# Earlier dilation start, half-graph blocks, first removals inside the slots and later chunk stores in a fused four-layer graph kernel

## The chip, the cores and the metric

The kernel runs on one core of one Trainium2 chip. The metric is the device time of one execution in microseconds (us), lower is better; a time without a profile is the median of several runs. A core has TensorE (PE; its weight loads are listed as PEld), VectorE (DVE), ScalarE (ACT), GpSimd (POOL), and a queue, SP, from which most plain transfers are issued. GpSimd's queue issues transfers too: here all those that change the type of the data.

## The reference, cut to what matters

There are 16 graphs of 1024 nodes with 128 features, and four layers with a layer norm behind each. Layer 0 is attention masked by the adjacency; layer 1 a maximum over neighbours; layer 2 a sum over neighbours with a two-stage perceptron; layer 3 first thins out ("dilates") the adjacency row by row and then runs three passes of neighbour means and a batch norm over all graphs.

```python
def _dilate_pattern(adj_bool, mask_b):
    def step(carry, n):
        row = jnp.take(carry, n, axis=0)
        nbi = row.astype(jnp.int32)
        num = jnp.sum(nbi)
        sf = jnp.where(num > T_DIL, (num + K_DIL - 1) // K_DIL, 1)
        rank = jnp.cumsum(nbi)
        rm = row & (rank % sf == 0)
        valid = (mask_b[n] != 0) & (num > 1)
        rm = jnp.where(valid, rm, False)
        keep = ~rm
        carry = carry.at[n].set(row & keep)
        carry = carry.at[:, n].set(carry[:, n] & keep)
        return (carry, None)
    out, _ = jax.lax.scan(step, adj_bool, jnp.arange(N))
    return out
...
x = _layernorm(x + _L0_gnn_ref(x, adj, Wv, bv, Wk, bk, Wq, bq))
x = _layernorm(x + _L1_gnn_ref(x, adj, W, b))           # max over j of relu(p_i + q_j + b) * adj_ij
x = _layernorm(x + _L2_gnn_ref(x, adj, nodemask, W1, b1, W2, b2, eps))
x = _layernorm(x + _L3_gnn_ref(x, adj, nodemask, ...))  # dilate(adj), then 3 x (sage, relu, batch norm)
```

The dilation depends on the adjacency alone, not on the features, so it can run beside layers 0 to 2. But row n of a graph depends on the removals of all rows before it.

## The kernel before, in words

**Stages.** A prologue computes graph 0's attention. Then a loop of *slots* computes layer 1 for all graphs, and in its gaps layers 0 and 2 and the dilation. After the slots a *bridge* finishes layer 2 of the last graph and begins layer 3, and a tail does layer 3's three passes.

**Slots (L927).** `for s in range(-2, B * NP)`: each graph has NP = 86 slots, 1376 in all, and each slot has two halves of 512 nodes. In a half, `look_up` (L843) makes four TensorE products into one of two PSUM tiles `pg`, and VectorE takes the running maximum into `best` (L908). What the products need is prepared two slots ahead: `count` (product L812, ScalarE L813), `table` (L824, L827) and `low_part` (L832, L834). The subset counts read a chunk `AT` of the transposed adjacency; each chunk serves PC = 10 slots.

**Transfers in the slots.** `load_columns(at)` (L753) is called every ten slots, for a chunk two chunks ahead. It issues the load of chunk `at` on GpSimd (L764, float32 to fp8, four buffers), and on SP the store of the chunk before it, `at - 1`, to `adj8` (L758), from which layer 3 reads later. `load_x` (L747) fetches the features of the next graph on SP, in three buffers; `load_rows` (L751) the adjacency rows `An` on GpSimd.

**Streams.** Other work is written as generators: `attend` and `scores` (layer 0 of the next graph), `tables_of` (layer 1's tables), `rest` (norm of layer 1 and all of layer 2 for the graph before). At each step a generator yields `ask(engine, cost, ...)`. `advance` lets it go on when there is `room` on that engine in this half slot, when its delay is over, and when one of the two shared PSUM banks is free. So the order on each engine is written at build time by costs, not by measured times.

**Dilation (generator `dilation`).** It runs over K = 32 blocks of R = 32 rows, for all 16 graphs at once. For a block, VectorE prepares counts (`spread`, `low_counts`, `rest`, L655), then GpSimd runs a chain of 31 rows (L669 to L679), 10 small instructions each, every row depending on the one before. The result `hit` goes to DRAM and back in another layout on SP (L686, L689), VectorE transposes it to `hit_T` (L703), GpSimd computes thresholds (L707 on), and the next block can begin. In `remove`, four column groups per block follow: TensorE ranks (L599), ScalarE `rank` (L601), VectorE `gone` (L613, two buffers), SP stores of `gone` to `removed` (L615) and of a transposed part to `removed_T` (L622). `prepare` loads and counts the block after.

`dilate_on` (called once in each half slot) takes the dilation's next step once `due` is no later than the present slot, and adds to `due` what the step yields: 1.03 slots for a row, and for the yield ahead of `hit_T` a number that makes a whole block last `(B * NP - 10) / K` = 42.69 slots. `due` starts at 0, so block 0 begins in slot 0.

**What sets the order of the work.** In the slots and the bridge, TensorE, ScalarE, VectorE and GpSimd run in the order written (`manual_schedule`). SP is not on that list: the scheduler orders SP's transfers itself when the kernel is built, by its own estimate of when each can go. [...]

**Bridge (L930 to L975).** When the slots are over, the rest of the dilation generator is run, its pool is closed, `first_weights` loads layer 3's weights, `load_near` and `load_gone` fetch the stored adjacency of graphs 0 and 1 and the removals of graph 0. `rest(B - 1)` is taken in pieces (`go_on(n)`), with graph 0's removals between: `both_halves` (products L1008 and L1010 into `pgone`, VectorE `near` L1014), then `degrees` (L1026, ACT copy L1027), `expanded` (fp8 to float32 copies, L1050), `settle` (1/degree on VectorE), and behind the last norm six chunks of graph 1.

Of the kernel before, what the change touches and what calls it, by code (L numbers as in the profile page):

```python
# [40 lines left out]
P = 128  # L41
T = N // P
# [32 lines left out]
def tile_graph_layers(ctx: ExitStack, tc, a, out):  # L75
# [166 lines left out]
    def layers_012():  # L242
# [3 lines left out]
        psum = psums.enter_context(tc.tile_pool(name="psumA", bufs=1, space=PSUM))  # L246
        apool = es.enter_context(tc.tile_pool(name="apool", bufs=1))
        w4 = es.enter_context(tc.tile_pool(name="w4", bufs=1))
        dil = right.enter_context(tc.tile_pool(name="dil", bufs=1, side="right"))
        w2 = right.enter_context(tc.tile_pool(name="w2", bufs=1, side="right"))  # L250
        steps = dil.tile([P, 512 + P], BF, name="steps")
        nc.vector.memset(steps, 1.0)
        upto, beyond = steps[:, :512], steps[:, P:]
# [246 lines left out]
        def dilation():  # L500
# [134 lines left out]
            for k in range(K):  # L635
# [59 lines left out]
                if k + 1 < K:  # L695
# [2 lines left out]
                    at = dil.tile([P, Q, R], F32, name="at_columns", tag="far")  # L698
                    nc.vector.tensor_tensor_scan(at.rearrange("p q m -> p (q m)"), running.rearrange("p q m -> p (q m)"),
                                                 near.rearrange("p q m -> p (q m)"), 0.0, op0=ALU.mult, op1=ALU.add)  # L700
                yield (B * NP - 10) / K - 36.93, 0.65, False
                hit_T = dil.tile([P, Q, R], BF, name="hit_T")
                nc.vector.transpose(hit_T.rearrange("p q m -> p (q m)"), hit_p.rearrange("p q m -> p (q m)"))  # L703
                cut(E[:, :, own], hit_T, counts[:, 3, :])
# [37 lines left out]
            for cost, gives in behind:  # L742
                yield 0.5, cost, gives

        def load_x(b):
            X[b] = apool.tile([P, T, D], F32, name="X", bufs=3)
            nc.sync.dma_start(out=X[b], in_=x[b].rearrange("(t p) d -> p t d", p=P))  # L747
# [4 lines left out]

        def load_columns(at):  # L753
            b, c = divmod(at, T + 1)
            if at:
                before, k = divmod(at - 1, T + 1)
                rows = min(CH, N - k * CH)
                nc.sync.dma_start(out=adj8[before][k * CH:k * CH + rows], in_=AT[at - 1][:rows])  # L758
            if b < B:
                rows = min(CH, N - c * CH)  # L760
                t = AT[at] = apool.tile([CH, N], F8, name="AT", bufs=4)
                if rows < CH:
                    nc.gpsimd.memset(t, 0.0)
                nc.gpsimd.dma_start(out=t[:rows], in_=adjT[b, c * CH:c * CH + rows])  # L764
# [89 lines left out]
        def dilate_on():  # L854
            nonlocal due, wants_bank
            if due <= now and not (wants_bank and taken >= 2 and given.get(taken - 2, 1e9) > now):
                after, cost, wants_bank = next(dilate, (B * NP, 0, False))
                due += after
                room["V"] -= cost

        def slot(s, last):

            nonlocal now
            now = s
            b, g = divmod(s, NP)
            if s >= 0 and g == 0:
                bests[b] = bests[b - 1] if b else w4.tile([P, 2, N], F32, name="best")
                if b + 1 < B:
                    start(tables_of(b + 1), True)
                    load_x(b + 1)  # L870
                    start(attend(b + 1))
                    start(scores(b + 1))
            if s >= 0 and g % PC == 0 and b * (T + 1) + g // PC + 2 <= B * (T + 1):
                load_columns(b * (T + 1) + g // PC + 2)
            for h in range(2):
                now = s + 0.5 * h
                for e in ROOM:
                    room[e] = min(room[e] + ROOM[e] / 2, ROOM[e] / (2 if e in ("PE", "V") else 1))
                if s >= 0:
                    pg = psum.tile([P, 2, 512], F32, tag="wide", name="pg", bufs=2)  # L880
                    look_up(s, h, pg)
                early = s >= 0 and due < now
                if early:
                    dilate_on()
                advance(("PE",))
                advance(("A", "V", "Pool"))
                if s >= 0 and not early:
                    dilate_on()
                if h == 0 and s % 2 and s + 1 < last:
                    low_part(s + 1)  # L890
                if s + 2 < last:
                    count(s + 2, h)
                    if h and s % 2 == 0:
                        table(s + 2)
                if s >= 0:
                    own = bests[b][:, :, halves[h]]
                    if g == 0:
                        if b:
                            if h:
                                merge(b - 1, h)  # L900
                            total(b - 1, h)
                        nc.vector.tensor_copy(own, pg)
                        if b and h:
                            start(rest(b - 1))
                    else:
                        if g == NP - 1 and h:
                            merge(b, 0)
                        nc.vector.tensor_max(own, own, pg)  # L908
            if s >= 0:
                hots.pop(s)  # L910

        dilate = dilation()
        due, wants_bank = 0.0, False
        load_x(0)
        for at in range(2):
            load_columns(at)
# [1 line left out]
        for t in range(T):  # L918
            while ("e", 0, t) not in happened:
                next(front)  # L920
            for what in back:
                if what[5] == ("e", 0, t + 1):
                    break
        for _ in front:
            pass
        first = tables_of(0)
# [3 lines left out]
        with tc.manual_schedule(engines={mybir.EngineType.PE, mybir.EngineType.Activation, mybir.EngineType.DVE,  # L930
                                         mybir.EngineType.Pool}):
            for s in range(-2, B * NP):
                slot(s, B * NP)
            total(B - 1, 0)
            merge(B - 1, 1)
            total(B - 1, 1)
            assert not streams, streams
            for _ in dilate:
                pass
            right.close()  # L940
            first_weights()
            nears[0], nears[1] = load_near(0), load_near(1)
            gones[0] = load_gone(0)
            last = rest(B - 1)

            def go_on(n):
                for _ in range(n):
                    next(last, None)

            def both_halves(b, c):  # L950
                p = psum.tile([P, 2, 512], F32, tag="wide", name="pgone", bufs=2)
                for h in range(2):
                    removals(p[:, h], b, c, h)
                keep(b, nears[b][:, c, :], p.rearrange("p a n -> p (a n)"))

            go_on(27)
            for c in range(T):
                both_halves(0, c)
            go_on(5)
            nc.sync.dma_start(out=kept[0], in_=nears[0])  # L960
            gones[1] = load_gone(1)
            go_on(18)
            p = psum.tile([P, 2, 512], F32, tag="wide", name="pdeg", bufs=2)
            degrees(0, [p[:, h] for h in range(2)])
            go_on(12)
            expanded(0, range(T))
            go_on(12)
            settle(0)
            for _ in last:
                pass  # L970
            for c in range(6):
                both_halves(1, c)
            psums.close()
            psum = ctx.enter_context(tc.tile_pool(name="psum", bufs=2, space=PSUM))

# [40 lines left out]
    def one_half(b, i):  # L1016
# [2 lines left out]
        removals(p, b, c, h)  # L1019
        keep(b, nears[b][:, c, halves[h]], p)  # L1020

    def degrees(b, ps):
        deg = ep.tile([1, N], F32, name="deg")
        for p, s in zip(ps, halves):
            for c in range(T):
                nc.tensor.matmul(p, ones_b, nears[b][:, c, s], start=(c == 0), stop=(c == T - 1))  # L1026
            nc.scalar.copy(deg[:, s], p[0:1, :])  # L1027
        nc.sync.dma_start(out=degree[b], in_=deg)
        d = dues[b] = ep.tile([T, P], F32, name="deg_t", bufs=2)
        nc.sync.dma_start(out=d, in_=degree[b].rearrange("(t i) -> t i", t=T))  # L1030
# [15 lines left out]
    def expanded(b, chunks):  # L1046
        m = ms.setdefault(b, [])
        for c in chunks:
            m.append(ep.tile([P, N], F32R, name="m", bufs=10))
            nc.scalar.copy(m[c], nears[b][:, c, :])  # L1050
        return m

# [135 lines left out]
        nc.sync.dma_start(out=hidden[l][b], in_=R3[b])  # L1188
        nc.sync.dma_start(out=around[b], in_=convolve(r, m, part))

    ep = None
    Wr = Wx = bs = gs = bes = Wl = bl = None

    def first_weights():
        nonlocal ep, Wr, Wx, bs, gs, bes, Wl, bl
        ep = ctx.enter_context(tc.tile_pool(name="ep", bufs=1, side="right"))
        Wr, Wx, bs, gs, bes = ([f(f"L3_gnn_{w}{l}", pool=ep, queue=nc.sync) for l in (1, 2, 3)] for w, f in (
            ("Wr", weight), ("Wx", weight), ("b", column), ("g", column), ("be", column)))
        Wl = weight("L3_gnn_Wl", (P, 3, P), ("(c p) o -> p c o", {"p": P}), ep, nc.sync)
# [112 lines left out]
    def summed(b):  # L1312
        hs = []
        for l in range(2):
            r = ep.tile([P, N], F32, name="m", bufs=10)
            nc.sync.dma_start(out=r, in_=hidden[l][b])
            hs.append(r)
        p = wide("pl")
# [7 lines left out]
    o = summed(0)  # L1326
    for b in range(B):
        following = summed(b + 1) if b + 1 < B else None
        xb = ep.tile([P, T, D], F32, name="xb", tag="m", bufs=10)
        nc.sync.dma_start(out=xb, in_=x3[b])  # L1330
        for h in range(2):
            p = rows_bank("pback")
# [38 lines left out]
```

## Time and profile before

| | us |
|---|---|
| three runs | 6195.82, 6211.70, 6206.11 |
| median | 6206.11 |
| the profiled execution, its own time | 6199.75 |
| its span in the trace | 6198.0 |
| first look-up product (L843) / first maximum (best) | 133.2 / 140.0 |
| last maximum of the slots ends | 5088 |
| first neighbour product of layer 3 (L1071) begins | 5159.9 |
| tail from there to the end | 1038 |

The whole slot stage takes most of the time: 1376 slots in 4955 us. Its engines, per stretch (start and end in us, length, then busy us and number of instructions of PE, PEld, DVE, ACT and POOL, then TensorE's granted clock, the share of the DMA engines, GB/s). The four stretches are a piece of the first two graphs, one of graph 8, one of graph 11 and one of the last:

```profile
200.00:550.00 350.00, 316.24 (x1731) 167.12 (x1742) 306.55 (x434) 241.06 (x453) 246.86 (x863) 0.95 0.22 27
2624.00:2925.00 301.00, 278.45 (x1590) 148.90 (x1597) 268.48 (x400) 214.00 (x410) 215.91 (x724) 1.00 0.23 33
3538.00:3863.00 325.00, 287.11 (x1591) 153.01 (x1597) 268.76 (x400) 212.07 (x409) 219.98 (x730) 0.94 0.20 30
4798.00:5089.00 291.00, 242.99 (x1254) 111.98 (x1257) 240.53 (x290) 173.34 (x325) 182.25 (x622) 0.91 0.09 20
```

In the profile, L12 is line 12 of the kernel; `out<-in` are tile names; `x` is a number of instructions. A wait is listed as "engine line <- who ended the wait". Idle time of an engine that is not on the path to the end costs nothing.

### The profile page before, as it was taken

What the parts mean: (1) busy time and instruction counts of PE and PEld (TensorE: products, weight loads), DVE (VectorE), ACT (ScalarE), POOL (GpSimd) and SP (SyncE); (2) the same over time, 40 slices, a digit from 0 to 9 for tenths busy, and PEclk for the clock granted to TensorE, in tenths of its full rate; (3) what the DMA queues carried; (4) which work ended last, traced back from release to release, by engine and by line L of the source; (5) the groups of instructions that cost most, each with busy time, mean ns of one, the idle gap of its engine ahead of it and who ended that gap; (6) DMA issues with size and microseconds to landing.
All of it is one profiled execution on the core that took longest, in us unless ns stands there. A gap on an engine that the chain in (4) does not pass through costs nothing.

```text
span 6198.0 us, 93287 instructions
## 1 busy us (share of the span) xinstructions
PE 5582.7 (90%) x30144; PEld 3046.0 (49%) x30250; DVE 4870.0 (79%) x7484; ACT 3988.2 (64%) x7362; POOL 3613.1 (58%) x11879
## 2 busy tenths in 40 slices
PE   5989899989898989999989798989999878999998
PEld 4545454545454545454545454545444435555654
DVE  3888788888888888889888788888889875555455
ACT  3767676767676767677767576767666554344855
POOL 2676666667666767677777757667677651110114
PEclk8999999989999999999999899999999989999999
DMA  5021213121212212122121211212121014554645
GB/s 42 11 33 25 40 22 42 22 40 24 40 24 31 32 32 32 32 32 38 26 43 22 39 24 31 31 31 33 31 33 28 19 41 124 159 144 133 214 163 191
DMA packets 496976, 334.28 MB, mean 54 GB/s; under 512 B 303338, under 2 KB 448228, under 8 KB 492388
## 3 DMA queue, kind: packets, MB, share of 16 engines
q1 hardware_dynamic: 405504, 260.29, 14.5%
q0 software_dynamic: 89008, 67.42, 12.6%
q8 instruction: 237, 3.88, 0.3%
q14 instruction: 255, 2.09, 0.1%
q10 hardware_dynamic: 1972, 0.59, 0.1%
HBM read 362.38 MB, written 133.96 MB: 80 GB/s over the span
## 4 chain that ended last, share of the span: by engine, by line
PE 31%; DVE 10%; ACT 4%; POOL 3%; issue 2%; DMA 1%; SPq 0%; DVEq 0%; POOLq 0%; ACTq 0%
PE pg L843 7%; PE pagg L1071 5%; DVE best L908 5%; PE pm L812 3%; PE po L1101 2%; PE po L1095 1%; PE pa L439 1%; PE pav L397 1%; PE pp L300 1%; ACT hot L813 1%; PE pdeg L1026 1%; DVE near L1014 1%; PE psc L349 1%; PE prank L599 1%; PE pe L387 1%
## 5 line engine op out<-in xcount | busy, mean ns | idle before, releaser
L908 DVE TENSOR_TENSOR best<-best,pg 128x1024 f32<-128x1024 f32 x2720 | 3259.3, 1214 | 512.6 <-PE pg L843 501.7
L813 ACT ACTIVATE hot<-pm,one_less 128x512 fp32r<-128x512 f32 x2752 | 1887.4, 689 | 780.5 <-PE pm L812 773.2
L843 PE MATMUL pg<-hot,high 64*128 64x512 f32 x5504 | 1407.3, 508 | 258.9 <-DVE best L908 220.8
L843 PE MATMUL pg<-hot,low 64*128 64x512 f32 x5504 | 1115.5, 402 | 0.0
L812 PE MATMUL pm<-AT,lit 120*128 120x512 fp8e4 x2752 | 1085.9, 395 | 4.5 <-ACT low L834 3.5
L843 PEld LDWEIGHTS pg<-hot,high 64*128 64x128 f32 x5504 | 523.5, 187 | 1014.6 <-DVE best L908 492.8
L669 POOL TENSOR_SCALAR sc<-low_counts,half_mask,rest 16x1 f32<-16x1 f32 x992 | 354.4, 357 | 393.9 <-DVE rest L655 283.2
L843 PEld LDWEIGHTS pg<-hot,low 64*128 64x128 f32 x5504 | 537.9, 192 | 0.0
L812 PEld LDWEIGHTS <-lit 120*128 120x128 fp8e4 x2752 | 270.3, 98 | 389.8 <-issue 313.5
L674 POOL TENSOR_SCALAR sc<-sc 16x1 f32<-16x1 f32 x992 | 393.1, 396 | 105.1
L834 ACT CAST low<-pt 128x256 fp32r<-128x256 f32 x688 | 256.0, 372 | 263.3 <-PE pt L832 261.9
L671 POOL TENSOR_SCALAR sc<-sc 16x1 f32<-16x1 f32 x992 | 324.5, 327 | 107.6
L1116 POOL TENSOR_TENSOR length<-length,mhalf 128x8 f32<-128x8 f32 x48 | 78.9, 1644 | 489.2 <-DVE length L1115 489.2
L676 POOL TENSOR_SCALAR hit<-V,sc 16x31 bf16<-16x31 bf16 (+30 forms) x992 | 362.4, 365 | 0.0
L677 POOL TENSOR_SCALAR last_rank<-V,sc 16x31 f32<-16x31 bf16 (+30 forms) x992 | 342.9, 346 | 0.0
L832 PE MATMUL pt<-high,less 128*128 128x256 f32 x688 | 279.2, 406 | 67.6 <-ACT high L827 61.5
L824 PE MATMUL pt<-ident,sub 128*128 128x128 f32 x1376 | 277.5, 283 | 51.8 <-ACT hot L813 50.0
L486 DVE TENSOR_TENSOR sub<-sub,q 128x24 f32<-128x24 f32 (+11 forms) x768 | 304.0, 397 | 24.8 <-ACT q L304 10.4
L397 PE MATMUL pav<-v,eT 128*128 128x128 f32 x2048 | 301.5, 292 | 2.0 <-ACT eT L390 2.0
L397 PEld LDWEIGHTS pav<-v,eT 128*128 128x128 f32 x2048 | 255.4, 196 | 73.3 <-issue 55.7
L670 POOL TENSOR_SCALAR sc<-sc 16x1 f32<-16x1 f32 x992 | 237.0, 239 | 86.5
L349 PE MATMUL psc<-kT,qT 128*128 128x256 f32 x1024 | 276.3, 388 | 9.9 <-issue 9.9
(270 smaller groups left out, 9662.9 us busy)
## 6 DMA issues: line engine op xcount, KB each, us to landing
removed<-gone SPq DMA_DIRECT2D x128, 256.0 KB
An<-in_adj_dram POOLq DMA_DIRECT2D x16, 1024.0 KB, 16.0
E<-in_adj_dram POOLq DMA_DIRECT2D x128, 128.0 KB, 6.6
gone_all<-removed POOLq DMA_DIRECT2D x64, 256.0 KB, 10.2
near<-adj SPq DMA_DIRECT2D x16, 1024.0 KB
kept<-near SPq DMA_DIRECT2D x16, 1024.0 KB
share<-share SPq DMA_DIRECT2D x32, 512.0 KB
hidden<-r SPq DMA_DIRECT2D x32, 512.0 KB
```

The costliest lines, as they stand in the source:

```text
L349: nc.tensor.matmul(psc[:, 256 * i:256 * (i + 1)], qT[:, t * P:(t + 1) * P], kT[:, s.start + 256 * i:s.start + 256 * (i + 1)], start=False, ...
L397: nc.tensor.matmul(pav, eT[:, c, :], values[b][:, c, :], start=(c == 0), stop=(c == T - 1))
L669: gp.tensor_scalar(half, mine, half_mask[:, m], rest[:, n:n + 1], op0=ALU.mult, op1=ALU.add)
L671: gp.tensor_scalar(sf, half, 5.5, sf, op0=ALU.is_gt, op1=ALU.mult)
L674: gp.tensor_scalar(to, at, sf, none, op0=ALU.subtract, op1=ALU.subtract)
L676: gp.tensor_scalar(hit[:, n, n + 1:], V[:, n, n + 1:], at, None, op0=ALU.is_equal)
L677: gp.tensor_scalar(last[:, n + 1:], V[:, n, n + 1:], to, None, op0=ALU.is_le)
L812: nc.tensor.matmul(pm, lit[:, r, :], AT[b * (T + 1) + c][:, halves[h]], start=True, stop=True)
L813: nc.scalar.activation(hots[s][:, halves[h]], pm, AF.Relu, bias=one_less)
L843: nc.tensor.matmul(pg[:, a], part[rows, at * P:(at + 1) * P], hots[s][rows, halves[h]], start=(k == 0), stop=(k == 1))
L908: nc.vector.tensor_max(own, own, pg)
L1071: nc.tensor.matmul(pa[:, s], piece[:, t, :], m[c][:, s], start=(i == 0), stop=(i == 15))
```

## The change

It has four parts.

1. **Dilation starts in the prologue.** The first steps of block 0 (its load, `prepare`, and all 31 rows) are issued beside graph 0's attention: three steps after each of the eight attention tiles, and the remaining 11 behind the last GpSimd instruction of the prologue's norm (`behind` sets that order for the scheduler). `due` now starts at 13.0.
2. **A block lasts half a graph.** The pace is NP / 2 = 43 slots in place of 42.69.
3. **First removals in the last graph's slots.** When the dilation generator ends, a stream `first_removals` is started: it closes the dilation's pool, calls `first_weights` (which now loads `near` of graphs 0 and 1 ahead of the weights), loads the removals of graph 0 and does them in 16 half chunks, then the degrees, then 12 half chunks of graph 1 and `settle(0)`, as far as `advance` finds room; what is left runs behind the last norm in the bridge. The bridge keeps layer 2's `rest` without removals between. So that the pools can be opened in this order, `w2` moves to the other side of the memory, and the tiles `m` come from a pool of their own, `mp`.
4. **Later chunk stores.** `load_columns(at)` stores chunk `at - 2` in place of `at - 1`.

```diff
+        tops = es.enter_context(ExitStack())
+        w2 = tops.enter_context(tc.tile_pool(name="w2", bufs=1))
         dil = right.enter_context(tc.tile_pool(name="dil", bufs=1, side="right"))
-        w2 = right.enter_context(tc.tile_pool(name="w2", bufs=1, side="right"))
...
-                yield (B * NP - 10) / K - 36.93, 0.65, False
+                yield NP / 2 - 36.93, 0.65, False
...
+        def first_removals():
+            right.close()
+            first_weights()
+            pieces = [(0, i) for i in range(2 * T)] + [(1, i) for i in range(12)]
+            for n, (b, i) in enumerate(pieces):
+                if i == 0:
+                    gones[b] = load_gone(b)
+                    yield ask("PE", 0)
+                yield ask("PE", 0.5, take=True, delay=0 if i else 5)
+                p = shared("pgone")
+                removals(p, b, *divmod(i, 2))
+                yield ask("V", 0.7, give=True, same=True)
+                keep(b, nears[b][:, i // 2, halves[i % 2]], p)
+                if n == 2 * T - 1:
+                    nc.sync.dma_start(out=kept[0], in_=nears[0])
+                    deg = None
+                    for h in range(2):
+                        yield ask("PE", 1.8, take=True)
+                        p = shared("pdeg")
+                        degree_products(0, p, h)
+                        yield ask("A", 0.6, give=True)
+                        deg = degree_copy(0, p, h, deg)
+                    degree_turn(0, deg)
+                    happened["edges", 0] = now
+                if n == len(pieces) - 3:
+                    settle(0)
...
         def load_columns(at):
             b, c = divmod(at, T + 1)
-            if at:
-                before, k = divmod(at - 1, T + 1)
+            if at > 1:
+                before, k = divmod(at - 2, T + 1)
                 rows = min(CH, N - k * CH)
-                nc.sync.dma_start(out=adj8[before][k * CH:k * CH + rows], in_=AT[at - 1][:rows])
+                nc.sync.dma_start(out=adj8[before][k * CH:k * CH + rows], in_=AT[at - 2][:rows])
...
+                if after == B * NP:
+                    start(first_removals())
...
-            if s >= 0 and g % PC == 0 and b * (T + 1) + g // PC + 2 <= B * (T + 1):
+            if s >= 0 and g % PC == 0:
                 load_columns(b * (T + 1) + g // PC + 2)
...
-        due, wants_bank = 0.0, False
+        due, wants_bank = 13.0, False
...
         for t in range(T):
             while ("e", 0, t) not in happened:
                 next(front)
+            for _ in range(3):
+                next(dilate)
             for what in back:
                 if what[5] == ("e", 0, t + 1):
                     break
+        begin = len(nc.cur_bb.bb.instructions)
+        normed = [i for i in nc.cur_bb.bb.instructions if i.engine == mybir.EngineType.Pool][-1]
+        for _ in range(R + 3 - 3 * T):
+            next(dilate)
+        behind(normed, begin)
...
-            for _ in dilate:
-                pass
-            right.close()
-            first_weights()
-            nears[0], nears[1] = load_near(0), load_near(1)
-            gones[0] = load_gone(0)
+            tops.close()
+            expansions()
+            while ("edges", 0) not in happened:
+                next(streams[0])
             last = rest(B - 1)
...
-            go_on(27)
-            for c in range(T):
-                both_halves(0, c)
-            go_on(5)
-            nc.sync.dma_start(out=kept[0], in_=nears[0])
-            gones[1] = load_gone(1)
-            go_on(18)
-            p = psum.tile([P, 2, 512], F32, tag="wide", name="pdeg", bufs=2)
-            degrees(0, [p[:, h] for h in range(2)])
-            go_on(12)
+            go_on(62)
             expanded(0, range(T))
-            go_on(12)
-            settle(0)
             for _ in last:
                 pass
-            for c in range(6):
-                both_halves(1, c)
+            for stream in list(streams):
+                for _ in stream:
+                    pass
```

`degrees` is split into `degree_products`, `degree_copy` and `degree_turn`, with the same instructions; `first_weights` gains the line that loads the two `near` tiles, which left the bridge.

## The prediction, made before the changed kernel was run

> **What bounds the kernel now.** I read the page's busy times, then its groups.
>
> ```profile
> PE 5582.7 (90%) x30144; PEld 3046.0 (49%) x30250; DVE 4870.0 (79%) x7484; ACT 3988.2 (64%) x7362; POOL 3613.1 (58%) x11879
> ...
> L908 DVE TENSOR_TENSOR best<-best,pg 128x1024 f32<-128x1024 f32 x2720 | 3259.3, 1214 | 512.6 <-PE pg L843 501.7
> ```
>
> TensorE is the fullest engine; the maximum (L908) mostly waits for its products. The slots run from 133 us (first L843 product) to 5088 us (last maximum): 1376 slots in 4955 us, 3.60 us each. Cut at the first slot of each graph, graphs take 286 to 325 us; those without a long stall take about 304 us. So I listed every DVE pause over 2.5 us inside the slots: 147.6 us. Next, the waits of that stretch (total us, times, longest), then those of the DMA queue SP:
>
> ```profile
> DVE best L908 <- PE pg L843: 501.7, 848, 20.3
> ...
> DVE gone L613 <- DMA removed<-gone: 80.6, 9, 18.0
> ...
> PE ptr L290 <- DMA X<-in_x_dram: 28.7, 4, 20.3
> ...
> DVE hit_T L703 <- DMA hit_p<-hit: 23.6, 2, 14.4
> ```
>
> ```profile
> SPq L758 <- DMA AT<-in_adjT_dram: 2846.5, 138, 54.8
> SPq L686 <- POOL hit L678: 463.6, 24, 29.7
> SPq L615 <- DVE gone L613: 372.7, 47, 19.4
> ```
>
> The first list has three stalls that stop the slots; the second says why. The store of an adjacency chunk (L758) waits for its own load, 2846.5 us in 138 times. One place, on SP's timeline:
>
> ```profile
> 1280.10 0.45 SPq L758 DMA_DIRECT2D adj<-AT  x1
> 1280.65 0.54 SPq L615 DMA_DIRECT2D removed<-gone  x1
> 1281.28 0.41 SPq L622 DMA_DIRECT2D removed_T<-last_T  x1
> 1281.78 2.17 SPq L615 DMA_DIRECT2D removed<-gone  x1
> ```
>
> The chunk's load went out on GpSimd at 1277.1, late, because it stood in GpSimd's order among the dilation rows. The store left 3.0 us later, and the `removed` stores left in a burst behind it. As `gone` has two buffers, VectorE stood 9.1 us at L613. The X load of graph 12 shows the same on TensorE (last bracket: idle before it):
>
> ```profile
> 3561.55 1.11 PE L290 MATMUL ptr<-ident,X 128*128 128x128 f32 x4 [20.32 <-DMA X<-in_x_dram]
> ...
> 3564.53 1.22 DVE L908 TENSOR_TENSOR best<-best,pg 128x1024 f32<-128x1024 f32 x1 [20.30 <-PE pg L843]
> ```
>
> **What the Trainium skill says.** "PSUM — Partial Sum Buffer", Engine vs sequencer instructions: the three vector-like engines run their queues strictly in order and matmuls complete in program order. The trace agrees: one late X (20.32) stops unrelated products and maxima (20.30). "DMA: Bandwidth & Descriptors", SWDGE vs HWDGE vs iDMA: a DMA that casts can only be issued from GpSimd. So chunk loads (f32 to fp8) must share GpSimd's order with the rows; L764 is indeed on POOL, 0.66 us per issue. "TensorE: Matmul & The Clock Gate", What's actually happening: an idle window of about 3.4 us halves TensorE's clock until a busy one. The trace agrees: removal products after a 3.41 us pause at 5110.7 took 0.63 us, later ones 0.38.
>
> **Part by part, against the profiled run (6199.75; span 6198.0).** The median of the three runs, 6206.11, is 6.4 above it.
>
> *Later chunk stores.* Issue count is unchanged; each now needs a load issued 20 slots earlier, not 10. (AT has four buffers: a buffer is loaded again 20 slots after its store was issued, 71 us, so no new wait there.) I compared the order of SP's queue with the slots. A `removed` store can still be held by a chunk load younger than the point where it is needed; I call the distance slack, in slots. Before, nine blocks have slack of 0 or less, the nine with stalls: -4 cost 18.0, -3 11.8, -2 14.9, -1.5 7.4, -1 9.1, -0.5 4.8 and 5.8, 0 4.2, and one at the edge 4.7. After, only three blocks remain: slack +1 (4 by the row of 0), -2 (15 to 23), -4.5 (20 to 23, carried on from -4): 39 to 50, I take 47. Gain 80.6 - 47 = **33**. Bounds 20 and 81 (none left).
>
> *X loads.* Before, two stood behind a store whose load belongs to slot 0 of the graph that needs X: 20.3 + 8.7 = 29.0. After, X of graphs 4 to 15 stands behind a store whose load is issued at slot 80 of the graph before. GpSimd is then in a row block started near slot 62: 18 rows at 3.39 us (distance of successive L669) and two norms at 3.7 is 69 us against 59 us of slots, then landing, issues and X itself: ready near 81.5 us, needed near 82.6. Forecast gain **29**, and the small margin is priced two steps below.
>
> *Half-graph blocks.* The pace goes from 42.69 to 43 slots, and the start moves to a fixed phase: `hit_T` (L703) at slots 13 and 56 of every graph, where it drifted from 39 to 29.5 and from 81.5 to 72. Before, two blocks were late, 9.3 + 14.4. Blocks 1 and 31 get other phases. Gain **23**. A third stall, 8.7 at slot 18.5 of the last graph (ACT waiting for GpSimd's `left`, L431), has the rows in front of it and moves too: **9**.
>
> *What is late next.* GpSimd. A block of rows takes 31 x 3.39 = 105 us alone, 108 to 138 with norms, `left` and issues between; L703 then comes 5.3 us after the last row at the least (block 31). For blocks whose rows span slots 62 to 99, I count 121 us of GpSimd work against some 125 of slots: margin 4, uncertain by 5. With X's margin of 1 and 14 repeats, I take 1.4 us a graph, **+20**; bounds 0 and 60. DMAs moved past GpSimd's rows (chunk loads, E, An) keep their issue time, 0.7 to 1.0.
>
> *Block 0 in the prologue.* 24 of its steps run beside attention tiles, 11 behind the norm's last GpSimd instruction. GpSimd is two tenths busy in the page's first slice. Its 19 or 20 rows end near 121.5 us, `ln_st` arrives near 123, so they hide; were that cover gone, each row late is 3.4 us. On ScalarE, copies that wait for the second E block sit ahead of the first eT copies: some 6 us on attention; but before, the first maximum (140.0) waited for just that preparation at slot 0 (L642 behind L569), which is now gone. Net **0**, bounds -6 and +6.
>
> *Work added to the slots.* The new order puts 16 removals (0.43 us of TensorE, 0.69 of VectorE each, from the bridge) and 16 degree products (0.22) in the last 12.5 slots: TensorE 16 x 0.65 = 10.4, VectorE 16 x 0.69 = 11.0. They lie in the same slots, so one hides the other at best: 12 with losses; 2 if the last slots, whose other streams have ended, have room. The first removal waits for its `gone_all` rows, and the look-ups queue behind it on TensorE: 2. Together **+14**. SP's added issues there (`near`, weights, 0.4 us each) have nothing urgent behind them. I also assigned each instruction's duration to its half slot in both orders and summed the larger of TensorE and VectorE: the first graph, which had no removal step in its first 43 slots and now has, grows by 5 to 13, take **+5**, since its pauses of before cover some; the 14 others, whose steps now meet other half slots, by about 1 each, **+14**. Bounds of all these 15 and 45.
>
> *The bridge.* These lines are of the stretch after the slots (start, us):
>
> ```profile
> 5111.24 1.05 ACT L428 CAST parts<-left 128x1024 bf16<-128x1024 f32 x1 [2.23 <-POOL left L431]
> ...
> 5118.41 10.52 PE L439 MATMUL pa<-An,parts 128*128 128x512 fp8e4 x48
> ```
>
> Layer 2's product `pa` needs only `parts`, done at 5112.3, but stands behind the removals until 5118.4: -6.1. Degrees were 2 x 1.89 on TensorE plus a wait of 0.66: -4.4. `settle` is 1.4 of VectorE: -1.4. Against that a colder start of `pa` (the clock rule above; estimated from 0.63 against 0.38 on a few matmuls) 1.3, and a wait no longer hidden, about 1.6. **-9**, bounds -13 and 0. Graph 1's twelve removals stay behind the last norm, as before; w2 and m tiles only change place: 0.
>
> Sum: -33 - 29 - 23 - 9 + 20 + 14 + 5 + 14 - 9 = **-50**. From 6199.75 that is 6150, from the median 6156; I take 6153, between them.
>
> **Rivals.** *More gain.* `gone` waits vanish and GpSimd keeps pace: 28 of the 47 go too, and the 20 do not come: -50 - 28 - 20 = -98, **6105**. For it: SP's order is built ahead of the run, and the three blocks' slack is only a count of slots. Against: slack predicted all nine stalls.
>
> *Nothing left.* The stores are delayed, but 40 to 80 us of small GpSimd waits spread over all graphs replace nine large ones: **6200**. For it: the sum of pauses under 2.5 us is untouched by the change, and VectorE still has 512.6 us ahead of L908. Against: no single place for it.
>
> *Slower: a late chain in every graph.* The fixed phase repeats one alignment some 15 times. If GpSimd's rows end behind L703 or hold the slot-80 load by more than the margin, VectorE or TensorE stops in each graph: at 7 us a graph in place of 1.4, 15 x 5.6 = 84 more, -50 + 84 = +34, **6237**. It decides from 50 / 15 = 3.3 us more a graph (4.6 to be seen as slower). For it: margins of 1 and 4 us; blocks as long as 138 us occur. Against: chains before ended 5.3 to 21.5 us ahead of L703, with little loss in 30 blocks of 32.
>
> **Chances.** Forecast (6120 to 6185) 0.55; more gain 0.12; nothing left 0.18; slower 0.15. The range 6100 to 6215 leaves out half of the second and most of the fourth, 0.19. A change of 0.3% (19 us) is about what this measurement can tell from none: faster is below 6187, 0.66; within, 0.19; slower, 0.15.
>
> **What would show it.** Waits of L613 for `removed` fall from 80.6 to about 47, in blocks 0, 1 and 30; L290's wait for X falls from 28.7 to under 10; graphs settle near 304 to 307 us; the first maximum stays near 140; `pa` begins about 24 us after the last maximum instead of 30. I am wrong if graphs 2 to 14 each show a pause at the same slot (13, 56 or 0), or if SP's L758 holds other stores than these.

## The result, and the profile after

| | before | after |
|---|---|---|
| median, us | 6204.49 (4 runs) | 6251.25 (4 runs, 6248.33 to 6261.22) |
| ratio, 95% interval | | 1.0085, 1.0068 to 1.0101 |
| profiled execution, its own time / span | 6199.75 / 6198.0 | 6248.33 / 6246.6 |

The change makes the kernel slower, where some 50 us faster was forecast. The medians differ by 47 us, which is 0.75%; the ratio of 0.85% in the table is the estimate over all runs. On the page after, VectorE and GpSimd are within 16 us of their old busy time, but TensorE is busy 58 us longer (5582.7 before):

```profile
PE 5640.6 (90%) x30125; PEld 3073.5 (49%) x30250; DVE 4884.8 (78%) x7498; ACT 4009.2 (64%) x7362; POOL 3628.2 (58%) x11879
...
L938 DVE TENSOR_TENSOR best<-best,pg 128x1024 f32<-128x1024 f32 x2720 | 3262.7, 1213 | 535.3 <-PE pg L871 521.8
```

Where the 48.6 us between the two spans came from, cut at the same events in both traces (the start of the first maximum, then the end of a graph's last maximum; before, the last one of the slots starts at 5088 and ends at 5089.3):

| stage | before | after | difference |
|---|---|---|---|
| prologue, to the first maximum | 140.0 | 147.1 | +7.1 |
| slots of graph 0 | 286.3 | 312.2 | +25.9 |
| slots of graphs 1 to 14 | 4371.3 | 4381.6 | +10.3 |
| slots of graph 15 | 291.6 | 305.9 | +14.3 |
| bridge, to the first L1101 (L1071 before) | 70.7 | 59.6 | -11.1 |
| tail | 1038.1 | 1040.2 | +2.1 |

The pauses that the prediction counted did go. VectorE's pauses over 2.5 us in the slots sum to 147.6 us before and 87.0 after. These are the waits in the slots after (total us, times, longest us):

```profile
DVE best L938 <- PE pg L871: 521.8, 921, 6.1
...
DVE gone L614 <- DMA removed<-gone: 48.6, 4, 21.7
DVE e L353 <- PE psc L350: 40.5, 34, 5.3
DVE sub L483 <- PE pt L852: 37.5, 55, 1.0
...
ACT off L338 <- DMA An<-in_adj_dram: 25.3, 11, 4.6
```

The wait for `removed` is 48.6 us (80.6 before; 47 forecast), and the longest wait for products 6.1 (20.3). But the total in front of the maximum did not fall (501.7 before): 60.6 us of long pauses are gone, and the slots are 50.5 us longer all the same. Some 111 us have come in small pieces, 96 of them in graphs 1 to 14 (10.3 us longer, with 86.0 us less of long pauses). SP's own waits say that one part of the change did not take place:

```profile
SPq L786 <- DMA AT<-in_adjT_dram: 2518.0, 144, 47.7
SPq L616 <- DVE gone L614: 752.4, 63, 23.3
```

SP still waits for the chunk loads, all 144 times. A store leaves 4.0 us after the issue of its own load in the median; before it was 3.9. Ten slots later would have been some 36 us more.

What the small pieces are is seen in one graph. This is graph 8, which had no pause over 2.5 us before and a single one, of 3.1 us, after; each line gives start and end, length, and busy us of TensorE, its weight loads, VectorE, ScalarE and GpSimd, then TensorE's clock. First before, then after:

```profile
2624.90:2926.20 301.30, 278.46 (x1593) 148.91 (x1599) 268.78 (x400) 213.65 (x409) 216.26 (x725) 1.00 0.23 33
```

```profile
2637.70:2951.40 313.70, 291.23 (x1588) 154.53 (x1595) 269.48 (x398) 214.53 (x408) 215.12 (x720) 0.95 0.22 33
```

The same work takes 12.4 us more, with TensorE's clock at 0.95 in place of 1.00. In the trace after, gaps of TensorE (stretches without a product) return at the same slots in nearly every graph. At slot 81 (here graph 9), VectorE has four steps of the dilation's `prepare` and the first tables of the next graph in one half slot, 2.0 us between two maxima:

```profile
3242.29 1.21 DVE L938 TENSOR_TENSOR best<-best,pg 128x1024 f32<-128x1024 f32 x1
3243.42 0.41 DVE L545 TENSOR_TENSOR_SCAN U<-running,upper 128x128 bf16<-128x128 bf16 x1
3243.87 0.23 DVE L549 TENSOR_TENSOR upper<-upper,square_T 128x128 bf16<-128x128 bf16 x1
3244.13 0.32 DVE L551 SCALAR_TENSOR_TENSOR far<-U,upper 128x128 f32<-128x128 bf16 x1
3244.48 0.23 DVE L553 TENSOR_SCALAR Vp<-far 128x128 bf16<-128x128 f32 x1
3244.68 0.08 DVE L483 MEMSET sub<- 128x24 f32 x1
3244.79 0.74 DVE L487 TENSOR_TENSOR sub<-sub,q 128x24 f32<-128x24 f32 x3
3245.45 1.21 DVE L938 TENSOR_TENSOR best<-best,pg 128x1024 f32<-128x1024 f32 x1
...
3246.71 0.50 PE L871 MATMUL pg<-hot,high 64*128 64x512 f32 x2 [2.03 <-DVE best L938]
```

With two `pg` tiles TensorE cannot run further ahead, and stands 2.03 us. Others: at slot 16 attention's exponential (L360) stands behind four ScalarE steps of the dilation (L733, 1.33 us), which come three slots after `hit_T`, and TensorE waits 1.7 us; one of 1.46 us follows at slot 19, behind ScalarE's `high` (L855). At slot 8 the scores wait for the adjacency rows, whose load GpSimd issued between two rows of the chain:

```profile
3283.40 1.03 POOL L779 DMA_DIRECT2D An<-in_adj_dram  x1 [1.95 <-issue]
...
3297.44 1.15 ACT L338 ACTIVATE off<-An,ones 128x1024 bf16<-128x1024 fp8e4 x1 [4.62 <-DMA An<-in_adj_dram]
...
3298.64 0.58 PE L349 MATMUL psc<-off,penalty 128*128 128x512 bf16 x1 [4.68 <-ACT off L338]
```

Of graphs 4 to 13, all ten have the gaps at slots 16, 19 and 81, and eight the one at slot 8 (over 1.3 us each).

### The profile page after: what moved, and what is told of

Read it like the earlier page. It is cut to its first block, busy times and chain, and to the rows that moved or that the text cites. A ratio compares the mean times of both kernels' runs of the same rounds, so it can differ in the third digit from the quotient of the medians.

```text
span 6246.6 us, 93303 instructions
## 1 busy us (share of the span) xinstructions
PE 5640.6 (90%) x30125; PEld 3073.5 (49%) x30250; DVE 4884.8 (78%) x7498; ACT 4009.2 (64%) x7362; POOL 3628.2 (58%) x11879
## 3 DMA queue, kind: packets, MB, share of 16 engines
q1 hardware_dynamic: 405504, 260.29, 14.3%
## 4 chain that ended last, share of the span: by engine, by line
PE 56%; DVE 17%; ACT 10%; POOL 8%; DMA 5%; issue 4%; SPq 0%; DVEq 0%; ACTq 0%; POOLq 0%
PE pg L871 16%; DVE best L938 9%; PE pm L840 6%; PE pagg L1101 5%; PE pav L398 4%; PE psc L350 3%; DMA An<-in_adj_dram 3%; ACT hot L841 3%; PE pp L301 2%; PE pa L440 2%; DVE sub L487 2%; PE prank L600 2%; PE po L1131 2%; PE pe L388 1%; PE pt L860 1%
## 5 line engine op out<-in xcount | busy, mean ns | idle before, releaser
L871 PE MATMUL pg<-hot,high 64*128 64x512 f32 x5504 | 1425.9, 515 | 209.0 <-DVE best L938 190.4
L871 PE MATMUL pg<-hot,low 64*128 64x512 f32 x5504 | 1131.5, 408 | 0.0
L840 PE MATMUL pm<-AT,lit 120*128 120x512 fp8e4 x2752 | 1103.4, 401 | 6.4 <-ACT low L862 6.3
L871 PEld LDWEIGHTS pg<-hot,high 64*128 64x128 f32 x5504 | 531.0, 189 | 981.6 <-DVE best L938 446.4
L871 PEld LDWEIGHTS pg<-hot,low 64*128 64x128 f32 x5504 | 548.1, 196 | 0.0
L675 POOL TENSOR_SCALAR sc<-sc 16x1 f32<-16x1 f32 x992 | 394.8, 398 | 105.0
L672 POOL TENSOR_SCALAR sc<-sc 16x1 f32<-16x1 f32 x992 | 330.2, 333 | 107.7
L852 PE MATMUL pt<-ident,sub 128*128 128x128 f32 x1376 | 281.8, 287 | 23.1 <-ACT hot L841 21.4
## 6 DMA issues: line engine op xcount, KB each, us to landing
An<-in_adj_dram POOLq DMA_DIRECT2D x16, 1024.0 KB, 14.3
gone_all<-removed POOLq DMA_DIRECT2D x64, 256.0 KB, 10.8
```

Source lines behind the costliest of these rows:

```text
L675: gp.tensor_scalar(to, at, sf, none, op0=ALU.subtract, op1=ALU.subtract)
L840: nc.tensor.matmul(pm, lit[:, r, :], AT[b * (T + 1) + c][:, halves[h]], start=True, stop=True)
L871: nc.tensor.matmul(pg[:, a], part[rows, at * P:(at + 1) * P], hots[s][rows, halves[h]], start=(k == 0), stop=(k == 1))
```

## The experiments

**Is it the stores?** Two runs: part 4 added alone to the kernel before (shown), and part 4 taken back from the changed kernel (the reverse).

```diff
-                before, k = divmod(at - 1, T + 1)
+                before, k = divmod(at - 2, T + 1)
...
-    ... in_=AT[at - 1][:rows])
+    ... in_=AT[at - 2][:rows])
```

> The kernel before with part 4 alone (chunk stores ten slots later). Theory (part 4 removes the queue stalls, the rest of the change costs time): the waits of L613 for removed and of L290 for X, 80.6 + 28.7 us before, fall to under half, and the time falls by 30 to 80 us, to 6125 to 6175. Rival (the phase of the blocks, not the store, took the stalls away): the two waits stay above 80 us together and the time is within 15 us of 6204.

> The changed kernel with part 4 undone (chunk stores as before, parts 1 to 3 kept). Theory (part 4 pays): the wait of the gone step for removed rises from 48.6 us to 90 or more, and the time by 30 to 80 us, to 6280 to 6330. Rival (the phase alone took the stalls away): wait and time stay within 15 us of 48.6 and 6251.

Alone: 6207.57, ratio 1.0003 (0.9995 to 1.0010), no change. The two waits are as before:

```profile
SPq L758 <- DMA AT<-in_adjT_dram: 2861.4, 138, 55.5
```

```profile
DVE gone L613 <- DMA removed<-gone: 86.3, 10, 18.5
PE ptr L290 <- DMA X<-in_x_dram: 27.7, 4, 19.6
```

Taken back: 6267.16, ratio to before 1.0092 (1.0075 to 1.0109) against the changed kernel's 1.0085; the intervals overlap, and the wait for `removed` stays at 48.7. (The median is 16 us from the changed kernel's, 1 us more than its rival allowed.) In the main both rivals were right: part 4 as written has no effect that shows, and something else took the stalls away.

**Is it the pace, or a single late load?** In what follows, *phase* means the slots of a graph at which `hit_T` falls. In the first kernel part 2 is undone, so that the phase drifts again; in the second the load of An is asked for earlier.

```diff
-                yield NP / 2 - 36.93, 0.65, False
+                yield (B * NP - 10) / K - 36.93, 0.65, False
```

```diff
-            load_rows(b)
+            if b not in An:
+                load_rows(b)
...
+            if s >= 0 and g == NP - 6 and b + 2 < B:
+                load_rows(b + 2)
```

> The changed kernel with part 2 undone: a block lasts 42.69 slots, so its phase against the graph drifts by 10 slots over the run where it was fixed. Theory (a fixed phase repeats the same small collisions in each graph: TensorE idle 2.0 us at slot 81 in 15 graphs, 1.6 to 4.7 at slot 8 in nine, 1.7 at slot 16 in twelve, and a halved clock behind them): these gaps move and some go; the time falls by 10 to 50 us, to 6200 to 6240. Rival (the added work and the denser slots cost the time, whatever the phase): within 8 us of 6251. Third: other slots collide as often, with the stalls of the queue back: 6255 to 6290.

> The changed kernel with one edit: the adjacency rows An of a graph are loaded six slots before the end of the graph ahead of the one in which they were asked for, far from the row chain that delays the load on GpSimd. Theory (the late An is one of the recurring costs: 25.3 us of waits at slot 8, and some 7 us of halved clock behind it in eight graphs): that wait goes to nearly 0 and the time falls by 25 to 45 us, to 6206 to 6226. Rival (the slots are full there anyway, the time shows up at the next wait): 0 to 10 us.

Drifting pace: 6326.65, ratio 1.0188 (1.0173 to 1.0203). None of the three expectations had that: `hit_T` drifts from slot 13 to slot 4 (and from 56 to 46), where the row chain is late for `hit_T` (39.6 us in six waits) and X comes 31 and 38 us late in two graphs. Earlier An: 6347.15, 1.0217 (1.0202 to 1.0232), worse by 96 us than the changed kernel, which neither expectation had. The wait for An is gone, but X is now late in 13 graphs (the same waits seen at the weight loads and at the products):

```profile
PEld ptr L291 <- DMA X<-in_x_dram: 118.3, 13, 18.9
PE ptr L291 <- DMA X<-in_x_dram: 110.3, 13, 18.4
```

An's issue (1.04 us) now stands right ahead of slot 80's chunk load on GpSimd, and X's load on SP stands behind that chunk's store (both are seen in the timeline). Moving one load cost 96 us where 25 to 45 were to be saved, so I varied the phase itself.

**Is it the phase?** Four kernels in which only numbers of the pacing differ (the first edit is of the kernel before, once with -5.0 and once with 17.0; the second of the changed one, once with 9.0 and once with 29.0):

```diff
-                yield (B * NP - 10) / K - 36.93, 0.65, False
+                yield NP / 2 - 36.93, 0.65, False
...
-        due, wants_bank = 0.0, False
+        due, wants_bank = -5.0, False
```

```diff
-        due, wants_bank = 13.0, False
+        due, wants_bank = 9.0, False
```

> The kernel before with two numbers changed: a block lasts 43 slots and due starts at -5, so that L703 falls at slots 34 and 77 of every graph; all else as before, block 0 begins in slot 0. In the kernel before, the graph with these phases had no long pause and took 301 us. Theory (the phase decides: 34 and 77 is a good one, 13 and 56 a bad one): graphs of 299 to 308 us, no repeated gap over 2 us, a slot stage of 4840 to 4900 us against 4949, and 6120 to 6170 in all, although the last block ends five slots later. Rival (any fixed phase repeats some stall in all graphs): one stall of 3 to 20 us comes back at one slot in ten or more graphs, and the time is 6220 to 6350.

> The kernel before with a block of 43 slots and due starting at 17, so that L703 falls at slots 56 and 13, the two slots of the changed kernel, with nothing else of the change. The dilation then ends some 25 slots after the last slot, so the bridge must grow by 60 to 130 us; the slots of the graphs in between are what counts. Theory (the fixed phase alone makes the changed kernel's graphs long): graphs 3 to 13 take 308 to 318 us each, as in the changed kernel (308 to 318), with idle gaps of TensorE at slots 8, 16 and 81. Rival (the phase needs the other parts to cost this): graphs of 300 to 306 us.

> The changed kernel with due starting at 9 in place of 13: L703 at slots 9 and 52 of every graph, all else the same. Theory (fixed phase, repeated collisions): the dilation's preparation no longer meets the next graph's first tables at slot 81, so that gap of 2.0 us goes, but the row chain is four slots nearer to L703 and An may be later; graphs change by 3 us or more each in one direction, so that the time is 30 us or more from 6251. Rival (the cost does not depend on phase): 6243 to 6259.

> The changed kernel with due starting at 29 in place of 13: L703 at slots 29 and 72, where the last graphs of the kernel before had it, all else the same; the first removals no longer fit into the slots and run in the bridge. Theory (the phase decides): graphs 1 to 14 take 300 to 308 us in place of 306 to 318, no gap at slots 8, 16 and 81; the slot stage falls by 60 to 130 us, the bridge grows by 5 to 15; 6130 to 6200. Rival (the denser order of the changed kernel costs this at any phase): graphs of 310 or more, 6245 or more.

| kernel | `hit_T` at slots | median, us | ratio, 95% interval | us a graph, 4 to 13 | of these, us in TensorE gaps over 1.3 us |
|---|---|---|---|---|---|
| before | 39 and 81.5, drifting to 29.5 and 72 | 6204 to 6213 | 1 | 311.5 | 8.2, most of it behind stalls |
| before, due -5 | 34, 77 | 6077.36 | 0.9801 (0.9781 to 0.9820) | 302.3 | 1.4 |
| changed, due 29 | 29, 72 | 6203.93 | 0.9990 (0.9978 to 1.0001) | 305.2 | 3.8 |
| changed | 13, 56 | 6251.25 | 1.0085 (1.0068 to 1.0101) | 313.1 | 7.6 |
| before, due 17 | 56, 13 | 6277.04 | 1.0105 (1.0085 to 1.0126) | 313.8 | 7.6 |
| changed, due 9 | 9, 52 | 6275.50 | 1.0118 (1.0099 to 1.0136) | 317.7 | 10.1 |

Two numbers make the old kernel 2% faster (6120 to 6170 had been expected), and two make it slower. With due 17 nothing of parts 1, 3 and 4 is there, and the graphs are as long as the changed kernel's, no slot differing by more than 0.31 us in the mean of graphs 4 to 13, with the same gaps (2.0 at slot 81 in all of graphs 4 to 13, 1.7 at slot 16 in all, 2.3 to 3.9 at slot 8 in six). The rest of its time is a bridge of 133.7 us, for the dilation ends late. So the phase alone makes graphs 4 to 13 long. It also takes most of the stalls for `removed` away: 20.6 us are left with due 17, in two waits. With due 9 the gap at slot 81 was to go; it stayed in nine of the ten graphs (1.3 to 1.9 us), and the waits for An grew to 52.1 us. With due 29 graphs 1 to 3 took 327 to 342 us (late X of 25 and 26 us among the pauses), so that it came out 4 us above its expectation. At 34 and 77 no stall came back in all graphs. Its waits in the slots:

```profile
DVE best L908 <- PE pg L843: 469.6, 837, 7.1
...
DVE hit_T L703 <- DMA hit_p<-hit: 11.8, 1, 11.8
DVE gone L613 <- DMA removed<-gone: 10.8, 4, 4.8
```

Between 302.3 and 313.1 lie 10.8 us a graph, and between the gaps 6.2. That a gap costs its own length is not shown, and the rest lies in shorter waits, which I could not name one by one. By place, the changed kernel's graphs lose 11.9 us in slots 16 to 33 and 6.9 in slots 64 to 85 against due -5, and win 7.9 in the others.

**Is it the clock?** In the changed kernel TensorE's clock is halved for 23.9 us from slot 81 on in each of graphs 7 to 13. Products were added there that compute nothing new (each is overwritten by the real count; `count` runs two slots ahead, so that g = 83 is issued in slot 81):

```diff
+            for _ in range(8 if (g, h) == (NP - 3, 1) else 1 if g >= NP - 2 or g < 2 else 0):
+                nc.tensor.matmul(pm, lit[:, r, :], AT[b * (T + 1) + c][:, halves[h]], start=True, stop=True)
             nc.tensor.matmul(pm, lit[:, r, :], AT[b * (T + 1) + c][:, halves[h]], start=True, stop=True)
```

> The changed kernel with work added and nothing removed: eight copies of the count product, overwritten by the real one, behind the products of slot 81, where TensorE stood idle 2.0 us in 15 graphs, and one copy in each half of slots 82 to 85: 16 more products of 0.22 us a graph. Theory (the halved clock of some 24 us from slot 81 on costs time): the clock stays up there, the half-clock total of the slot stage falls by 150 to 300 us from 519, and the time falls by 20 to 50 us, to 6201 to 6231. Rival (the halved clock is a sign of a slack TensorE and costs nothing): the clock stays up and the time is 6245 to 6260. Third: the clock falls all the same, and the copies cost 10 to 50 us.

The clock stayed up, as 20.6 us from slot 81 of graph 9 on show, first the changed kernel (clock 0.57), then this one (0.98):

```profile
3245.10:3265.70 20.60, 17.81 (x56) 7.28 (x57) 20.29 (x35) 9.79 (x23) 17.55 (x47) 0.57 0.42 96
```

```profile
3251.90:3272.50 20.60, 14.85 (x72) 5.54 (x70) 20.30 (x34) 10.16 (x23) 17.54 (x47) 0.98 0.41 97
```

The half-clock total of the slots fell from 493 to 283 us (the 519 of the expectation counts a window that lies mostly in the bridge), and the time did not: 6252.29, ratio 1.0076 (1.0061 to 1.0092). Nor did a gain there cancel against the cost of the added products: slots 81 to 85 took 20.7 us in both kernels, in the mean of graphs 4 to 13. VectorE is busy for 20.3 of the 20.6 us shown, so it is VectorE that sets the time there. The rival was right: in these slots the low clock, and the busy time that it adds to TensorE, is a sign of an engine that is not pressed. The half clock that is left, in shorter pieces at slots 0 to 2, 8, 16 and 19 above all, was not tested.

**Does SP's order matter after all?** The store is made to follow, in the order that the scheduler builds, the load of the chunk two further on; once in the kernel before, once with due -5 as well.

```diff
...
+                begin = len(nc.cur_bb.bb.instructions)
+                nc.sync.dma_start(out=adj8[before][k * CH:k * CH + rows], in_=AT[at - 2][:rows])
+                if b < B:
+                    behind(nc.cur_bb.bb.instructions[begin - 1], begin)
```

> The kernel before with the chunk store two chunks late as in part 4, and also made to follow, in the order that the scheduler builds for SP, the load of the chunk two further on; part 4 alone left the store right behind its own load (median 3.9 us after it, in both kernels). Theory (an SP queue held by a young chunk's load is what delays removed and X): SP's wait for AT falls from 2847 us to under 500, the waits for removed and X from 80.6 + 28.7 to under 30, and the time falls by 50 to 110 us, to 6095 to 6155. Rival (the stalls have another cause, such as the distance of two gone buffers): removed stays above 50 us, within 20 us of 6205.

> Both edits that are expected to gain, together: L703 at slots 34 and 77 from block 0 in slot 0 (6077 alone) and the store that truly follows two chunks later. Theory (at a good phase only some 8 us of waits for removed are left): 6060 to 6080. Rival (the moved stores meet other transfers): 6085 to 6120.

Alone: 6090.91, ratio 0.9810 (0.9787 to 0.9834). Stores leave 46 us after their loads in the median, and SP's waits have turned round (AT 2846.5 before):

```profile
SPq L615 <- DVE gone L613: 1835.7, 118, 55.4
SPq L765 <- DMA AT<-in_adjT_dram: 156.7, 18, 35.4
```

No wait for `removed` or X over 2.5 us is left, and graphs 1 to 14 sum to 4258.0 us against 4371.3. Graphs 4 to 13 take 304.4 us each, although the phase drifts as before: at the phases of these graphs (36 and 78.5 down to 30.5 and 73) it costs little once the stalls are gone. With due -5: 6078.61, 0.9789 (0.9768 to 0.9810), no better than due -5 alone. At slots 34 and 77 SP still waits 2328.5 us for chunk loads, but `removed` only 10.8, so these waits hold little that is needed soon. The two cures are for the same 2%, and either is enough. These are the fastest versions found.

**What do the other parts cost at a good phase?** The changed kernel with due 34; what then does not fit into the slots is run behind them.

> The changed kernel with due starting at 34, so that L703 falls at slots 34 and 77; block 0 is still done in the prologue, and the first removals run in the bridge, as the dilation ends behind the last slot. Theory (the other parts cost only the prologue's 7 to 9 us and some us of bridge): 6080 to 6125, graphs of 299 to 308 us. Rival (with block 0 done early, the first graphs meet other waits, as at slots 29 and 72, where graphs 1 to 3 took 327 to 342 us): 6150 or more, with long pauses in graphs 1 to 3.

6101.78, ratio 0.9827 (0.9804 to 0.9850): graphs 2 to 14 take 301 to 304 us, but the prologue takes 147.6 us (138.6 in the kernel before with due -5) and the bridge 94.6 (76.9). The theory holds. At this phase the rest of the change costs some 24 us (6101.78 against 6077.36). Part 3 was not run alone.

## Why the prediction was wrong

- **Later chunk stores, -33: right size (-32), wrong cause.** The sentence that fails is "each now needs a load issued 20 slots earlier, not 10". The edit changes where the store stands in the program, but SP is ordered by the scheduler, and the store stayed 4.0 us behind its own load. The mechanism behind it, a young chunk load that holds SP, is right: with stores that do follow late, graphs 1 to 14 became 113 us shorter in all, where 33 and 29 had been forecast for `removed` and X. My list of slack came from the order of the whole change, so it saw the three blocks that remain (5.8, 19.9 and 21.7 us), but it was the new phase that left only three: they stay with part 4 taken back (48.7).
- **X -29, `hit_T` -23, `left` -9: near.** The waits for X fell from 28.7 to 7.5 us (14.3 with part 4 taken back), `hit_T` from 23.6 to 6.3, and the third stall went.
- **GpSimd late, +20: right size, other place.** It came at An, with waits of 25.3 us on ScalarE, which the step had passed over with "keep their issue time". The issue did stay at 1.03 us; its place among the rows did not. That the two sizes agree is luck.
- **Graphs 1 to 14 at the new phase, +14, is the step that failed.** The prediction had "the 14 others, whose steps now meet other half slots, by about 1 each". Without the long pauses, graphs 1 to 14 grew by 96 us, 6.9 each. Summing durations in each half slot and taking the larger of TensorE and VectorE supposes that these two wait for nothing but the larger total. The measured gaps are waits for other engines and loads (ScalarE's four steps at slot 16, a load at slot 8) or for a burst of VectorE (six small steps at slot 81), with two `pg` tiles as the only slack. A fixed phase repeats each of them in nearly every graph. That the phase is the cause is shown by due 17; how the 6.9 us split over single waits stays open.
- **Prologue, 0 with bounds of 6: +7.1.** I let GpSimd run 19 or 20 rows ahead of the norm; it was 21, and the norm began 5.9 us after its input had ended (0.1 before):

```profile
124.36 0.29 DVE L278 BATCH_NORM_STATS2 ln_st<-y 128x6 f32<-128x128 f32 x1
...
127.36 0.32 POOL L670 TENSOR_SCALAR sc<-low_counts,half_mask,rest 16x1 f32<-16x1 f32 x1
130.52 0.20 POOL L225 TENSOR_TENSOR ln_mv<-ln_st 128x8 f32<-128x8 f32 x1
```

  Attention itself ended 7.5 us later (the same step was at 116.84 before), where 6 was forecast. So the first look-up product came 13.1 us later, and 6.0 of these were won back at slot 0, as forecast.
- **First graph +5, removals +14: about right** without long pauses, +9.5 and +10.5 (5.6 and a first wait of 4.9). **Bridge -9: -11.1**; `pa` began 16.5 us after the last maximum had ended, before 29.2, but with two of its 48 products; the others ran from 23.1 on, 6.1 us earlier than before, as forecast.

The sum that was forecast for the slots was -41; it is +50, and 82 of that difference of 91 is the one term. The slower rival (6237) had the repetition of one alignment right and its places wrong: it named `hit_T` and the slot-80 load behind X, the margins that I had counted, and these held.

## What to carry to other kernels

When a periodic side job is locked to the period of the main loop, each collision is paid in every period: vary the phase as a parameter and measure it before anything else is tuned, for here two numbers were worth 2%, and at the good phase the rest of the change cost time. Check in the trace that a moved transfer has moved: the distance from load to store told in one number that part 4 had not happened. A sum of busy times per slot did not price the change of phase here: it had 1 us a graph where 6.9 came. Look for waits between engines inside the slot as well.

## What was not expected of the hardware

The prediction quotes for TensorE's clock that an idle window of about 3.4 us halves it until a busy one. The trace after does not fit this: after a gap of about 2.0 us at slot 81 the clock stayed at half for 23.9 us in each of graphs 7 to 13, although TensorE was busy 21.5 to 23.0 us of these (pairs of L871 took 0.79 us in place of 0.50). What ends the half clock is not shown. And holding the clock up with 16 added products a graph moved the time by nothing that could be measured.
